# Query features of the late token blocks as four 32-row matmul groups in a decoder layer on Trainium2

## The chip, the cores and the metric

The kernel runs on one core of one Trainium2 chip, as one launch. The metric is the device time of that launch in microseconds (us), taken from timed runs. A separate profiled execution gives the traces that are read here. Engines are named as in the profile: PE is TensorE (PEld its weight loads), DVE VectorE, ACT ScalarE, POOL GpSimd, and SP the engine that issues most DMAs.

## What is computed

A decoder layer in float32 over `x` of 2 x 2048 tokens with 512 features: linear attention with a random feature map, then cross attention to a context of 154 keys, then a mixture of experts, each on a layer norm of its input and added to it. The part that matters is the first:

```python
def _elu1(x):
    return jnp.where(x > 0, x + 1.0, jnp.exp(x))
qkv = x @ w_qkv
q, k, v = jnp.split(qkv, 3, axis=-1)            # to 16 heads of 32
q_proj = _elu1(jnp.einsum('bhnd,hdf->bhnf', q, proj_matrix))   # 32 -> 128
k_proj = _elu1(jnp.einsum('bhnd,hdf->bhnf', k, proj_matrix))
kv = jnp.einsum('bhnf,bhnd->bhfd', k_proj, v)
attn = jnp.einsum('bhnf,bhfd->bhnd', q_proj, kv)
k_sum = k_proj.sum(axis=2)
z = 1.0 / (jnp.einsum('bhnf,bhf->bhn', q_proj, k_sum) + 1e-08)
out = (attn * z[..., None]).transpose(0, 2, 1, 3).reshape(b, n, d)
return out @ w_out + b_out
```

## The kernel before

The 4096 tokens are eight blocks `b` of 512 (`TB`); blocks 0 to 3 are the first batch and 4 to 7 the second, which are called the late blocks here. The 16 heads are four chunks `c` of four heads, so a chunk is 128 rows of features by 512 tokens.

Products are kept exact by splitting each operand into a high part in the type `float32r` and a low part, the remainder. `TERMS` names the three products that are summed: high by high, low by high, high by low. A full product over 128 rows thus is three matmuls (`product`, L148). For a head's features only 32 rows are contracted, so the three terms are stacked instead: `stack` (L292) loads a chunk's queries from DRAM (`qd`, which holds the high and the low part) three times, by three DMAs, into 96 partitions (high, low, high) of `qst`; `pst` holds `proj` in the order (high, high, low). One matmul of 96 rows then sums the three terms of one head (`query_features`, L479), into one bank `pqp` of the PSUM pool `sc`, which has four banks.

`features` turns a bank into `e_q`: two operations on ScalarE (L364, L365: relu and exp of the negated value), one on VectorE (L366), after which the bank is free. `numerators` and `denominators` multiply `e_q` with `kv` and with the key sums by plain float32 matmuls of 32 columns, the four heads each in its own quarter of the array's columns (`columns.matmul`, L230; `pn` and `pd`). `columns.matmul` also keeps the order of these among themselves as written.

Dense work (`Dense`) is a list of generators that give one matmul at a step; loops call `dense.fill(n)` to put n of them between the steps of the latency-bound work. Which instruction comes when on each engine is then settled by a scheduler when the program is built, engine by engine, from what is ready in its own estimate; each engine runs its list in order.

The first loop does the keys of all blocks and the queries of the early ones. The late blocks' queries run in a loop of 17 steps (L1346): per step one chunk's features, the chunk before it into `pn` and `pd`, a part of the attention output of earlier blocks (`attended`: POOL multiplies `num` by the reciprocals `zr` at L563, ScalarE casts the result to `at` at L564, VectorE takes the remainder at L118; `attention_out`: the matmuls `po_a`), and at the end the layer norm and the queries of the cross attention (`pt_x`, `xpq`). `xr_a` are tiles of `x` to which the output is added. Large tiles come from one pool of 17 buffers of 8 KB a partition (`eight`); a DMA into a tile waits for a free buffer. The DMAs of `qst`, `zr`, `xr_a` and the results all stand in SP's one queue.

Of the kernel before, what the change touches and what calls it, by code (L numbers as in the profile page):

```python
# [9 lines left out]
F32 = mybir.dt.float32  # L10
FR = mybir.dt.float32r
# [6 lines left out]
P = 128  # L18
D = 512
NC = D // P  # L20
H = 16
HD = 32
FEAT = 128
TB = 512
# [13 lines left out]
def decoder_layer(  # L38
# [26 lines left out]
    nc = tc.nc  # L65
    tokens = x.shape[0]
    nblk = tokens // TB
    bpb = nblk // batches
# [7 lines left out]
    sc = ctx.enter_context(tc.tile_pool(name="sc", bufs=SC, space=PSUM))  # L76
    dram = ctx.enter_context(tc.tile_pool(name="dram", bufs=1, space=DRAM))
    summed_up = ctx.enter_context(ExitStack())
    rows = ctx.enter_context(ExitStack())
# [18 lines left out]
    def eight(shape, dtype, name):  # L98
        return big.tile(shape, dtype, tag="b8", name=name)

    def half(name, dtype=F32):
        return work.tile([P, 512], dtype, tag="kp", name=name, bufs=9)
# [13 lines left out]
    def low(dst, src, hi, eng=None):  # L116

        (eng or nc.vector).tensor_tensor(dst, src, hi.bitcast(F32), ALU.subtract)  # L118

    def load_weight(w, name):  # L120
        raw = eight([P, NC, w.shape[1]], F32, f"raw_{name}")
        for k in range(NC):
            nc.sync.dma_start(out=raw[:, k], in_=w[k * P : (k + 1) * P, :])
        return [raw[:, k] for k in range(NC)]

    def split_weight(raw, name, busy=False):

        hi = eight([P, NC, D], FR, f"{name}_hi")
        lo = eight([P, NC, D], FR, f"{name}_lo")
        for k in range(NC):  # L130
            if isinstance(raw, list):
                part = raw[k]
            else:
                part = load_tile(raw, 0, k, name)
            if busy:
                nc.gpsimd.tensor_scalar(hi[:, k], part, 1.0, None, ALU.mult)
            else:
                nc.scalar.copy(hi[:, k], part)
            low(lo[:, k], part, hi[:, k], nc.gpsimd if busy or k % 2 else nc.vector)
        return hi, lo  # L140

    TERMS = ((0, 0), (1, 0), (0, 1))
# [90 lines left out]
    columns = Columns()  # L233

    def fl(k, f):
        return int((k + 1) * f + 1e-6) - int(k * f + 1e-6)
# [27 lines left out]
    def layernorm(d, b, at, xts, name):  # L264


        made = {}

        def values(t):
            if t == 0:  # L270
                xts[b] = new_xt(f"{name}{b}")
            made[t] = normalize(load_tile(d, at, t, f"{name}{b}_"), f"{name}{b}_{t}")
            yield from ()

        def turn(t):
            transposed(made.pop(t), xts[b], t, f"{name}{b}_{t}")
            yield
            yield

        return [values(t) for t in range(NT)], [turn(t) for t in range(NT)]  # L280
# [4 lines left out]
    def load_tile(d, b, t, name):  # L285
        xs = work.tile([P, D], F32, tag="xs", name=f"xs{name}{b}_{t}", bufs=5)
        nc.sync.dma_start(out=xs, in_=tile_of(d, b, t))
        return xs
# [3 lines left out]
    def stack(dst, d, parts=(0, 1, 0)):  # L292
        for r, part in enumerate(parts):
            nc.sync.dma_start(
                out=dst[r * HD : (r + 1) * HD].bitcast(F32),
                in_=d[part].rearrange("(h d) n -> d h n", d=HD),
            )
# [33 lines left out]
    raw = wk  # L331
    wk = [eight([P, NC, D], FR, f"wk_{i}") for i in ("hi", "lo")]
    for t in range(NT):
# [5 lines left out]
        b = nc.vector.tensor_tensor(lo, pt, hi.bitcast(F32), ALU.subtract)  # L339
        c = nc.scalar.copy(wk[0][:, t], raw[t])  # L340
        d = (nc.gpsimd if t % 2 else nc.vector).tensor_tensor(wk[1][:, t], raw[t], wk[0][:, t].bitcast(F32), ALU.subtract)
# [7 lines left out]
    low(pst[rest], praw[rest], pst[rest])  # L349
    wq = split_weight(load_weight(w_qkv[:, :D], "wq"), "wq")  # L350

    kvs, kszs, pkvs, kaccs, made_kv = [], [], [], [], []
    qd = [[dram.tile([2, P, TB], F32, name=f"qd{b}_{c}") for c in range(NC)] for b in range(nblk)]
    stks, vas, kps = {}, {}, {}
# [6 lines left out]
    def features(src, name, e=None):  # L361

        e = half(f"e_{name}") if e is None else e
        nc.scalar.activation(e, src, AF.Relu, scale=-1.0)  # L364
        nc.scalar.activation(e, e, AF.Exp, scale=-1.0)  # L365
        nc.vector.scalar_tensor_tensor(e, src, 0.0, e, ALU.max, ALU.add)  # L366
        return e
# [102 lines left out]
    qsts, qps, pds, nums, numd, zrs, zds, ats = {}, {}, {}, {}, {}, {}, {}, {}  # L470

    def load_queries(b, c):
        qsts[b, c] = eight([3 * HD, 4, TB], FR, f"qst{b}_{c}")
        stack(qsts[b, c], qd[b][c])

    def query_features(b, c, h):
        head = slice((4 * c + h) * FEAT, (4 * c + h + 1) * FEAT)
        pp = sc.tile([P, TB], F32, tag="sc", name=f"pqp{b}_{c}_{h}")
        nc.tensor.matmul(pp, lhsT=pst[:, head], rhs=qsts[b, c][:, h, :], start=True, stop=True)  # L479
        e = None  # L480
        if b < bpb and h:
            e = early.tile([P, TB], F32, tag="eq", name=f"eq{b}_{c}_{h}")
        qps[b, c, h] = features(pp, f"q{b}_{c}_{h}", e)

    def numerators(b, c):
        if c == 0:
            if b < bpb:
                numd[b] = dram.tile([P, NC, TB], F32, name=f"numd{b}")
            else:
                nums[b] = eight([P, NC, TB], F32, f"num{b}")  # L490
        pn = bank(f"pn{b}_{c}")
        for h in (3, 2, 1, 0):
            columns.matmul(
                pn[h * HD : (h + 1) * HD, :],
                lhsT=kvs[b // bpb][:, 4 * c + h, :],
                rhs=qps[b, c, h],
                start=True,
                stop=True,
            )
        if b < bpb:  # L500
            num = half(f"num{b}_{c}")
            nc.vector.tensor_copy(num, pn)
            dense.after(8, lambda: nc.sync.dma_start(out=numd[b][:, c], in_=num))
        else:
            nc.vector.tensor_copy(nums[b][:, c], pn)
# [42 lines left out]
    def load_reciprocals(b, c):  # L548
        two = pair_of(f"zr{b}_{c}").bitcast(F32)
        for h in range(4):  # L550
            nc.sync.dma_start(
                out=two[h * HD : (h + 1) * HD],
                in_=zds[b][h : h + 1, c : c + 2].to_broadcast([HD, 2, TB]),
            )
        for i in range(2):
            zrs[b, c + i] = two[:, i]
# [18 lines left out]
    def attention_outs(b):  # L575
        return [attention_out(b, t) for t in range(NT)]
# [190 lines left out]
    for s in range(ws_gate.shape[1] // F):  # L767
# [9 lines left out]
        out=before,  # L777
        in_=before,
# [527 lines left out]
    for n in range(nblk * per):  # L1306
        b, c, t = n // per, n // NT % NC, n % NT
# [32 lines left out]
            load_queries(*chunks[bpb * NC])  # L1340

    wout = split_weight(w_out, "wout")
    steps = chunks[bpb * NC :]

    ahead = {n if n < 13 else n + 2: ((n - 1) // 2, (n - 1) % 2 * 2) for n in range(1, 15)}
    for n in range(len(steps) + 1):  # L1346
        if n < len(steps):
            b, c = steps[n]
            if n + 1 < len(steps):
                load_queries(*steps[n + 1])  # L1350
        if n + 1 in ahead:
            load_reciprocals(*ahead[n + 1])
        if n == 7:
            ln, tr = layernorm(x1[0], 0, 0, qts, "x")
            dense.add(*ln[:3])
            ln = ln[3:]
        if n == 8:
            dense.add(*tr[:1], *ln, *tr[1:])
        if n == 11:
            dense.add(*(cross_query(0, i) for i in range(NC)))  # L1360
        for i in range(2):
            if n < len(steps):
                query_features(b, c, 2 * i)
                query_features(b, c, 2 * i + 1)
            dense.fill(fl(2 * n + i, 13 if n < 12 else 14))
            if n in ahead:
                attended(ahead[n][0], ahead[n][1] + i)
                if ahead[n][1] and i:
                    whole = ahead[n][0]
                    if whole < nblk - 2:  # L1370
                        dense.add(*attention_outs(whole))
                    if whole + 1 < bpb:
                        load_numerators(whole + 1)
            if n and i:
                columns.batch()
                numerators(*steps[n - 1])
                denominators(*steps[n - 1])
        if n == 10:
            xwq = split_weight(wq_t, "xwq")
        if n == 11:  # L1380
            open_early.clear()
            attending.close()
            res = attending.enter_context(tc.tile_pool(name="res", bufs=1))
            for i in range(NC):
                load_keys(0, i)
# [3 lines left out]
    steps = [(b, c, t) for b in range(nblk) for c in range(NC) for t in range(NT)]  # L1389
    for n in range(len(steps) + LAG + 1):  # L1390
        if n < len(steps):
            b, c, t = steps[n]
# [44 lines left out]
        if n > LAG:  # L1437
            b, c, t = steps[n - LAG - 1]
# [47 lines left out]
    for n, (group, u) in enumerate(todo3):  # L1486
# [14 lines left out]
        if n == LAST:  # L1501
            f0, f1 = finished(g, 0), finished(g, 1)
            d = downs
# [115 lines left out]
```

## Time and profile before

| | |
|---|---|
| timed runs, median of 3 | 2338.83 us (2337.85 to 2339.55) |
| profiled execution, its own time | 2335.7 us |
| span of its instructions | 2333.9 us |
| granted TensorE clock, mean | 0.986 |
| busy: PE, DVE, ACT, POOL | 96%, 72%, 47%, 53% |
| the 128 matmuls of L479, first and last start | 232.3 and 632.7 us |
| DMA, whole span | 498.23 MB |

A busy time is the sum of what an engine's instructions cover. Matmuls are pipelined: one starts before the one before it has ended, so a matmul's price in a stream is the distance between starts and not its length. Half of the matmuls of L479 are those of the late blocks; they lie from about 480 us on.

### The profile page before, as it was taken

To read this page: it belongs to the slowest core of one execution; us is meant where nothing else is said; L and a number is where in the kernel's file an instruction comes from. 1 tells how busy PE (TensorE), PEld (TensorE's weight loads), DVE (VectorE), ACT (ScalarE), POOL (GpSimd) and SP (SyncE) were. 2 spreads that over 40 slices of the span, in tenths; PEclk is the share of its full clock that TensorE was granted. 3 is DMA by queue.
4 is the path that set the end of the run, shared out by engine and by line. 5 is a ranking of instruction groups with operands and counts; after the bars stand their busy time and mean duration, and the time that the engine had idled before them with its cause. 6 is when DMAs were issued, how large, how long until landed. Compare 5 with 4: busy or idle time off the path is not lost.

```text
span 2333.9 us, 35151 instructions
## 1 busy us (share of the span) xinstructions
PE 2237.3 (96%) x11978; PEld 1733.5 (74%) x11978; DVE 1682.5 (72%) x2733; ACT 1104.6 (47%) x2598; POOL 1225.4 (53%) x1078
## 2 busy tenths in 40 slices
PE   7999999898899999999999999999999999999998
PEld 6888777655566776766787877888878888788887
DVE  6554555578577776778977777787797877877776
ACT  4555676756466766775343343222433223332221
POOL 5545433547475565553765554555484554755543
PEclk9999999999999999999999999999999999999999
DMA  6555778899974665566866657665557656575553
GB/s 212 181 171 173 208 210 228 241 260 263 255 211 141 172 179 159 166 197 218 293 235 229 241 184 299 225 225 221 176 193 294 242 211 233 180 280 207 203 191 129
DMA packets 201810, 498.23 MB, mean 213 GB/s; under 512 B 27739, under 2 KB 47579, under 8 KB 181695
## 3 DMA queue, kind: packets, MB, share of 16 engines
q1 hardware_dynamic: 199902, 489.89, 64.1%
q0 software_dynamic: 1728, 6.09, 0.9%
q8 instruction: 96, 1.57, 0.3%
q14 instruction: 84, 0.68, 0.1%
HBM read 351.30 MB, written 144.60 MB: 212 GB/s over the span
## 4 chain that ended last, share of the span: by engine, by line
PE 70%; DMA 13%; DVE 8%; POOL 3%; issue 3%; ACT 2%; SPq 1%; DVEq 0%; POOLq 0%; ACTq 0%
PE pg L1082 28%; PE pf L1195 11%; PE pk L148 3%; PE pq L148 3%; PE pv L148 3%; PE pf L148 3%; PE po_x L148 3%; PE xpq L148 3%; PE pp L402 2%; PE pc L745 2%; PE xpt L725 2%; PE pkv L230 1%; PE psc L693 1%; DMA zr<-zd 1%; DMA wds<-wdq 1%
## 5 line engine op out<-in xcount | busy, mean ns | idle before, releaser
L1082 PE MATMUL pg<-xo,wq 128*128 128x512 f32 x3360 | 826.0, 392 | 4.0 <-DMA wq<-wqs 1.1
L1082 PEld LDWEIGHTS pg<-xo,wq 128*128 128x128 f32 x3360 | 629.8, 188 | 145.6 <-ACT s L1093 3.4
L1216 DVE TENSOR_TENSOR sum<-sum,pf 128x512 f32<-128x512 f32 x376 | 250.7, 682 | 50.2 <-PE pf L1195 43.5
L407 POOL TENSOR_TENSOR kacc<-kacc,e_k 128x512 f32<-128x512 f32 x128 | 166.1, 1298 | 226.2 <-DVE e_k L366 204.5
L703 ACT ACTIVATE xe<-psc,nb 128x154 f32<-128x154 f32 x512 | 194.7, 404 | 64.9 <-DVE nb L700 49.3
L708 POOL TENSOR_TENSOR xe<-xe,sm 128x616 f32<-128x616 f32 x128 | 156.9, 1234 | 107.9 <-DVE sm L707 71.5
L1195 PE MATMUL pf<-ht,wdo 128*128 128x512 f32 x696 | 188.4, 395 | 10.8 <-DVE sum L1216 10.8
L1145 POOL TENSOR_TENSOR u<-u,gr 128x512 f32<-128x512 f32 x48 | 65.6, 1368 | 238.4 <-DVE u L1114 237.1
L366 DVE SCALAR_TENSOR_TENSOR e_k<-pp,e_k 128x512 f32<-128x512 f32 x128 | 87.3, 684 | 107.4 <-ACT e_k L365 101.5
L1195 PEld LDWEIGHTS pf<-ht,wdo 128*128 128x128 f32 x696 | 130.8, 189 | 41.4 <-DVE sum L1216 12.1
L1195 PE MATMUL pf<-hb,wdo 128*128 128x512 f32 x522 | 148.3, 399 | 0.0
L1113 ACT ACTIVATE u<-u 128x512 f32<-128x512 f32 x80 | 50.6, 633 | 201.7 <-DVE u L1102 201.4
L148 PE MATMUL pf<-wd,hp 128*128 128x512 f32 x528 | 133.6, 400 | 4.7 <-DVE mv_n L248 3.4
L700 DVE TENSOR_REDUCE nb<-psc 128x2 f32<-128x308 f32 x256 | 111.8, 467 | 32.5 <-PE psc L693 32.2
L148 PEld LDWEIGHTS pf<-wd,hp 128*128 128x128 f32 x528 | 99.4, 190 | 32.9 <-issue 6.3
L1102 DVE TENSOR_TENSOR u<-u,pg 128x512 f32<-128x512 f32 x160 | 108.3, 680 | 10.2 <-PE pg L1082 9.0
L1195 PEld LDWEIGHTS pf<-hb,wdo 128*128 128x128 f32 x522 | 98.2, 189 | 22.4 <-DVE sum L1216 0.8
L703 ACT ACTIVATION_READ_ACCUMULATOR xe<-psc,nb 128x1 f32 x512 | 111.5, 218 | 0.0
L364 ACT ACTIVATE e_k<-pp 128x512 f32<-128x512 f32 x128 | 76.8, 601 | 71.0 <-PE pp L402 62.8
L693 PEld LDWEIGHTS psc<-xkst,xst 96*128 96x128 f32 x512 | 76.5, 194 | 37.1 <-ACT xe L703 16.8
L693 PE MATMUL psc<-xkst,xst 96*128 96x154 f32 x512 | 90.4, 285 | 13.4 <-ACT xe L703 7.3
L402 PEld LDWEIGHTS pp<-pst,kst 96*128 96x128 f32 x512 | 75.7, 191 | 25.2 <-issue 8.6
(285 smaller groups left out, 5131.9 us busy)
## 6 DMA issues: line engine op xcount, KB each, us to landing
wq<-wqs SPq DMA_DIRECT2D x90, 1024.0 KB
wqs<-wq SPq DMA_DIRECT2D x30, 1024.0 KB
wdo<-wds SPq DMA_DIRECT2D x29, 1024.0 KB
kst<-kd SPq DMA_DIRECT2D x96, 256.0 KB
qst<-qd SPq DMA_DIRECT2D x96, 256.0 KB
xst<-xqd SPq DMA_DIRECT2D x96, 256.0 KB
wdo<-wds SPq DMA_DIRECT2D x29, 768.0 KB
kd<-khl SPq DMA_DIRECT2D x32, 512.0 KB
```

The lines of the kernel that those rows point to most:

```text
L148: nc.tensor.matmul(dst, lhsT=a, rhs=b, start=n == 0, stop=n == len(todo) - 1)
L366: nc.vector.scalar_tensor_tensor(e, src, 0.0, e, ALU.max, ALU.add)
L402: nc.tensor.matmul(pp[:, h], lhsT=stks[b, c][:, h, rows], rhs=pst[:, head], start=True, stop=True)
L407: nc.gpsimd.tensor_tensor(acc, acc, kp, ALU.add)
L693: nc.tensor.matmul(psc[:, i], lhsT=xsts[b, c][:, h, t * P : (t + 1) * P], rhs=ksts[bt, c][:, h, :], start=True, stop=True,)
L700: nc.vector.tensor_reduce(nb[:, two], psc, AX.X, ALU.max, negate=True)
L703: nc.scalar.activation(e[:, h, :], psc[:, i], AF.Exp, bias=nb[:, h : h + 1], accum_out=sm[:, h : h + 1],)
L708: nc.gpsimd.tensor_tensor(e, e, sm.unsqueeze(2).to_broadcast([P, 4, keys]), ALU.mult)
L1082: nc.tensor.matmul(pb, lhsT=w[:, p, i, k, :], rhs=xop[:, q, k, :], start=first and m == 0, stop=m == len(todo) - 1, skip_group_check=True,)
L1102: nc.vector.tensor_tensor(dst, dst, pb, ALU.add)
L1195: nc.tensor.matmul(banks[i], lhsT=w[:, p, i * P : (i + 1) * P], rhs=t[q], start=new and m == 0, stop=m == len(TERMS) - 1, skip_group_check ...
L1216: nc.vector.tensor_tensor(dst, dst, banks[i], ALU.add)
```

## The change

The late blocks' queries are no longer stacked. One DMA per chunk loads the pair (high, low) as it lies, 128 partitions by two parts by 512 tokens, and two chunks share one buffer (`qh`). Head `h` of a chunk then lies in partitions 32 h to 32 h + 31. `load_rows` makes a second copy of `proj` laid out in the same way, as high and low part (`prows`). `chunk_features` computes a chunk's four heads by twelve matmuls of 32 rows, three terms by four heads, each head in its own quarter of the array's rows and into its own bank, in the order term by term. All twelve are given at the first of a step's two halves; before, two heads were given in each half. The early blocks keep `query_features`.

```diff
+    def load_rows():
+
+        raw = eight([P, NC, FEAT], F32, "prow")
+        for h in range(4):
+            nc.sync.dma_start(
+                out=raw[h * HD : (h + 1) * HD],
+                in_=proj.rearrange("d (c h f) -> d h c f", c=NC, h=4)[:, h],
+            )
+        pair = eight([P, 2, NC, FEAT], FR, "prows")
+        nc.scalar.copy(pair[:, 0], raw)
+        low(pair[:, 1], raw, pair[:, 0], nc.gpsimd)
+        prows.append(pair)
...
     def load_queries(b, c):
+        if b >= bpb:
+            if c % 2 == 0:
+                two = eight([P, 2, 2, TB], FR, f"qh{b}_{c}")
+                for i in range(2):
+                    qsts[b, c + i] = two[:, i]
+                    nc.sync.dma_start(
+                        out=two[:, i].bitcast(F32), in_=qd[b][c + i].rearrange("r p n -> p r n")
+                    )
+            return
         qsts[b, c] = eight([3 * HD, 4, TB], FR, f"qst{b}_{c}")
         stack(qsts[b, c], qd[b][c])
...
+    def chunk_features(b, c):
+
+        pps = [sc.tile([P, TB], F32, tag="sc", name=f"pqp{b}_{c}_{h}") for h in range(4)]
+        for n, (i, j) in enumerate(TERMS):
+            for h in range(4):
+                rows = slice(h * HD, (h + 1) * HD)
+                columns.matmul(
+                    pps[h],
+                    lhsT=prows[0][rows, i, c, :],
+                    rhs=qsts[b, c][rows, j, :],
+                    start=n == 0,
+                    stop=n == 2,
+                    skip_group_check=True,
+                )
+        for h in range(4):
+            qps[b, c, h] = features(pps[h], f"q{b}_{c}_{h}")
...
     wout = split_weight(w_out, "wout")
+    load_rows()
     steps = chunks[bpb * NC :]
...
         for i in range(2):
-            if n < len(steps):
-                query_features(b, c, 2 * i)
-                query_features(b, c, 2 * i + 1)
+            if n < len(steps) and i == 0:
+                chunk_features(b, c)
             dense.fill(fl(2 * n + i, 13 if n < 12 else 14))
```

## The prediction

> **What bounds the kernel now.** I read the page's totals first, then the windows of the stage that is edited, then who waits there, then TensorE's timeline for the price of each kind of matmul.
>
> ```profile
> PE 2237.3 (96%) x11978; PEld 1733.5 (74%) x11978; DVE 1682.5 (72%) x2733; ACT 1104.6 (47%) x2598; POOL 1225.4 (53%) x1078
> ```
>
> TensorE is busy for 96% of the span, so time added to or taken from its stream anywhere reaches the end nearly one to one. The late blocks' query features run from about 490 to 640 us (windows view: stretch and its length, busy us of PE, PEld, DVE, ACT, POOL with counts, granted clock, DMA share, GB/s):
>
> ```profile
> 490.00:640.00 150.00, 136.13 (x687) 82.99 (x687) 104.50 (x159) 87.41 (x161) 82.85 (x75) 0.99 0.93 254
> ```
>
> Here TensorE stands still for 150.0 - 136.1 = 13.9 us, and the DMA engines are busy 0.93 of the time, against 0.65 over the span (the queues' shares on the page). The waits of this stretch (total us, times, longest):
>
> ```profile
> ACT at L564 <- POOL num L563: 30.5, 13, 6.6
> POOL num L563 <- DMA zr<-zd: 29.7, 4, 17.1
> ...
> PEld pqp L479 <- DVE e_q L366: 14.8, 14, 3.3
> ...
> PE pqp L479 <- DVE e_q L366: 8.1, 7, 2.5
> ```
>
> The reader sees a chain: late transfers (zr) hold POOL, POOL holds ScalarE's cast `at`, and the query features queued behind that cast free their banks late, so the next pqp matmul waits 8.1 us in all on TensorE. The prices come from TensorE's timeline (start, length, line, operation, count):
>
> ```profile
> 512.90 0.61 PE L148 MATMUL po_a<-wout_hi,at 128*128 128x512 f32 x2
> 513.36 0.39 PE L148 MATMUL po_a<-wout_lo,at 128*128 128x512 f32 x1
> 513.58 0.39 PE L148 MATMUL po_a<-wout_hi,at 128*128 128x512 f32 x1
> 513.90 1.06 PE L230 MATMUL pn<-e_q,kv 128*32 128x512 f32 x8
> 514.78 1.04 PE L230 MATMUL pd<-e_q,ksz 128*32 128x512 f32 x8
> 515.75 0.50 PE L148 MATMUL po_a<-wout_hi,at 128*128 128x512 f32 x1
> 516.09 0.40 PE L479 MATMUL pqp<-qst,pst 96*128 96x512 f32 x1
> 516.33 0.40 PE L148 MATMUL po_a<-wout_lo,at 128*128 128x512 f32 x1
> ```
>
> Starts count, not lengths. Full-array matmuls follow each other at 0.23 us, and the 96-row pqp is one of them (516.09 to 516.33 is 0.24). Going over to the column-tiled pn costs 513.90 - 513.58 = 0.32, that is 0.09 more. Eight of these (4 heads in 2 passes) take 0.88. Coming back costs 515.75 - 514.78 = 0.97, again 0.09 more, and the first matmul after it takes 0.34 to the next start, 0.11 more, since its weights were not loaded ahead. That tiles do run at once is seen in an earlier stretch of the same timeline:
>
> ```profile
> 481.56 0.63 PE L230 MATMUL pn<-eq,kv 128*32 128x512 f32 x3
> 481.58 0.62 PE L230 MATMUL pn<-e_q,kv 128*32 128x512 f32 x1
> 482.01 0.60 PE L230 MATMUL pn<-eq,kv 128*32 128x512 f32 x3
> ```
>
> Four start within 0.02 us, the next round 0.45 later.
>
> **Removed.** The 64 stacked pqp of the late blocks: 64 x 0.23 = 14.7 us of TensorE. Also 48 loads of 256 KB.
>
> **Added on TensorE.** 192 matmuls of 32 rows. No row of the trace shows a row-tiled one; bounds are four at once (0.23 a round, as the column tiles do) and one after another (0.23 each). I take the first, since the nearest row is the column-tiled one. In the order in which the built program issues them, the 192 do not stand in 16 blocks of twelve: they stand in 38 runs, 16 of nine to twelve, one of three and 21 single ones between po_a, pt_x or xpq matmuls, because each goes out when its bank is due. A long run still has three rounds: 16 x 3 x 0.23 = 11.0. The 22 short ones hide nothing: 22 x 0.23 = 5.1. The whole program's changes of tiling go from 288 to 341, 53 more. A change costs 0.09 of emptying and 0.11 of weights not loaded ahead, 0.20 together: 53 x 0.20 = 10.6. The bounds of this are 0 (rows of the array may need no emptying) and 0.20. Sum: 11.0 + 5.1 + 10.6 - 14.7 = +12.0 us.
>
> One rule would make it worse. The weight loads of pn stand together (start, length, count):
>
> ```profile
> 636.61 0.16 PEld L230 LDWEIGHTS pn<-e_q,kv 128*32 128x32 f32 x8 [0.35 <-issue]
> 637.07 0.13 PEld L230 LDWEIGHTS pd<-e_q,ksz 128*32 128x32 f32 x4 [0.30 <-issue]
> ```
>
> One lasts 0.11 (median 110 ns in the tile view of `ksz`), so four within 0.13 us are not one after another, and I let row tiles load at once too. The Trainium skill ("TensorE: Matmul & The Clock Gate", LDWEIGHTS) gives a load P / 1.2 ns with P its columns, 107 ns for 128 columns whatever the rows; twelve in series would be an estimated 1.28 us a chunk against the 0.92 removed. The same page (Measured speedup vs the span model) gives four row tiles of K=32, N=512 a speedup of 3.07 and not 4, an estimated 12 x 0.23 / 3.07 = 0.90 us a chunk in place of 0.69, which would add 3.4 us. No run here shows either.
>
> **Loads.** 16 of 512 KB and four of 64 KB for the rows of `proj` take the place of 48 of 256 KB: 12.6 to 8.7 MB, 3.9 of the stage's 38.14 MB:
>
> ```profile
> DMA packets 19844, 38.14 MB, mean 254 GB/s; under 512 B 3733, under 2 KB 3925, under 8 KB 19449
> ```
>
> At 0.93 x 150 = 139.5 us for 38.14 MB that is 14 us of DMA time, a share of 0.84. SP issues 28 loads fewer at 0.43 us each (median of qst in its line's view), and they stood ahead of zr and xr_a in its queue. What TensorE gets of it is bounded by 0 and its 13.9 us of standing; I take 4, half of the 8.1 that hang on late features, since the column of waits starts at zr but POOL's own 1.43 us per num remains.
>
> **Banks and features.** All four banks fill together, in the third round. ScalarE then has 8 operations at about 0.53 start to start (4.2 us), VectorE 0.68 after the last: 4.9 us until the fourth bank is free, 5.6 with the rounds. A chunk lasts 10.2 us now (pn at 503.79 and 13 chunks later at 636.61), so this is covered, except where the casts `at` come between: in the new order four stand in a row on ScalarE, paced by POOL (4 x 1.43 = 5.7), behind waits that now reach 6.6. What is queued behind the waiting cast is the next chunk's features, and behind those the pqp runs and all of TensorE. Two chunks need 2 x 5.6 + 5.7 - 1.2 = 15.7 of 20.4, which leaves 4.7; waits of 5 to 6.6 exceed it by 0.3 to 1.9. That is about what pqp waits today: I book 0 and keep 8 either way.
>
> **The first chunks.** Before, three matmuls of chunk (4,0) go out by 479.7. Now all twelve stand behind the second group of sums (491.9). Between them and (4,1) lie 12 xpv matmuls (2.8 us), then only 16 sums passes (1.8): with 4.9 needed each time TensorE waits 2.1 + 3.1 = 5.2, against 1.7 now (1.02 and 0.68 before the pqp at 496.3 and 497.5). +3 us. The copy and subtraction for `prows` (0.6 on ScalarE, 1.3 on POOL) lie before that beside other work; uncovered they cost 1.9. The bigger buffer costs nothing: two slots were cycling for qst, and prows takes the one that pst frees.
>
> **Sum.** +12.0 - 4 + 3 = +11 us on the profiled execution's 2335.7 us (span 2333.9): 2346.7. The three timed runs have their median 3.1 above that execution: about 2350; I write 2349.
>
> **Rivals.**
> 1. Faster: the changes of tiling are free for rows, and the lighter DMA queue decides. TensorE then pays 11.0 + 5.1 - 14.7 = +1.4, +3 at the start, and the waits give back up to 12: -8, 2331. For it: 0.93 DMA share and waits that begin at zr. Against it: the 0.09 at each change to columns. It decides from the point where a change costs below 0.05 us (53 x 0.05 = 2.7). 0.17.
> 2. No change: free or half-priced changes and 4 to 6 us back from the waits: 2336 to 2342. 0.17.
> 3. Rows in series (the change doesn't do what it says): 192 x 0.23 + 10.6 - 14.7 = +40, less 1 for the rest: 2378. Against it: the four starts within 0.02 us. 0.10.
> 4. My case, 2344 to 2366: 0.56.
>
> **The numbers.** About 0.2% (4.7 us) is what a measurement can tell from no change: faster is below 2334.2, slower above 2343.5. Slower is 0.56 + 0.10. The range runs from rival 1's 2331 to 2368, which is my case with the 3.4 and the 8 of late features added and part of the relief lost; left out are most of the serial case and a gain beyond 8.
>
> **What would show it.** Right: in the stretch that replaces 490 to 640, TensorE's timeline has pqp runs of twelve in about 0.7 us, single ones that cost 0.6 from the matmul before to the matmul after, DMA share near 0.84, and waits of pqp on e_q of 5 to 13 us. Wrong: starts 0.23 apart within one round (rival 3), single pqp with 0.23 on both sides (rival 1), or the waits on zr gone with the standing time under 5 us.

## The result

| | median | runs | TensorE busy | DMA moved |
|---|---|---|---|---|
| before | 2338.47 us | 2337.85 to 2339.55 | 2237.3 us | 498.23 MB |
| after | 2364.08 us | 2358.73 to 2369.06 | 2257.1 us | 494.30 MB |

The changed kernel takes 1.0113 of the time before, with a 95% interval of 1.0096 to 1.0129: 25.6 us more. The profiled execution of after took 2369.06 us (span 2367.3) and is the longest of its four; against the profiled one before (2335.7, span 2333.9) it is 33.4 us longer, so a difference between the two traces shows somewhat more than the medians do.

The page's totals after:

```profile
PE 2257.1 (95%) x12106; PEld 1737.2 (73%) x12106; DVE 1681.2 (71%) x2733; ACT 1101.7 (47%) x2599; POOL 1222.9 (52%) x1079
```

TensorE is busy 19.8 us longer and stands 13 us longer. The other engines do what they did. The windows view of the stage that was 490 to 640, now 497.5 to 677 (stretch and length, busy us of PE, PEld, DVE, ACT, POOL, granted clock, DMA share, GB/s):

```profile
497.50:677.00 179.50, 156.51 (x819) 87.80 (x818) 109.93 (x173) 86.81 (x167) 82.62 (x81) 0.92 0.65 203
```

The DMA share fell from 0.93 to 0.65, further than the 0.84 forecast, and yet TensorE stands for 23.0 us in place of 13.9. And the granted clock, 0.99 before, is 0.92. Two timeline excerpts of TensorE (start and length in us, line, operation, tiles, count) show the edit itself, a run of twelve and a single:

```profile
592.94 0.39 PE L148 MATMUL po_a<-wout_lo,at 128*128 128x512 f32 x1
593.26 0.97 PE L230 MATMUL pqp<-qh,prows 32*128 32x512 f32 x12
594.16 1.07 PE L230 MATMUL pn<-e_q,kv 128*32 128x512 f32 x8
...
529.99 0.61 PE L148 MATMUL po_a<-wout_hi,at 128*128 128x512 f32 x2
530.53 0.50 PE L230 MATMUL pqp<-qh,prows 32*128 32x512 f32 x1
530.96 0.50 PE L148 MATMUL po_a<-wout_lo,at 128*128 128x512 f32 x1
531.30 0.62 PE L148 MATMUL po_a<-wout_hi,at 128*128 128x512 f32 x2
```

Twelve take 0.90 from their start to the start of what follows: the four of a round start within 0.01 us, the second round 0.34 after the first, the third 0.23 after that, and `pn` 0.33 after the third. The single stands where two po_a would have gone on at 0.23: the second po_a of the first pair started at 530.22 (0.23 after the first), and the next but one after it starts at 531.30, which is 1.08 for what would take 0.46 without the pqp. It costs 0.62, and the prediction's 0.23 + 2 x 0.20 is 0.63.

### The profile page after: what moved, and what is told of

The parts are those of the page before. It is cut to its first block, busy times and chain, and to the rows that moved or that the text cites. A ratio compares the mean times of both kernels' runs of the same rounds, so it can differ in the third digit from the quotient of the medians.

```text
span 2367.3 us, 35401 instructions
## 1 busy us (share of the span) xinstructions
PE 2257.1 (95%) x12106; PEld 1737.2 (73%) x12106; DVE 1681.2 (71%) x2733; ACT 1101.7 (47%) x2599; POOL 1222.9 (52%) x1079
## 2 busy tenths in 40 slices
DMA packets 199825, 494.30 MB, mean 209 GB/s; under 512 B 27290, under 2 KB 47642, under 8 KB 179710
## 4 chain that ended last, share of the span: by engine, by line
PE 57%; DVE 5%; DMA 4%; POOL 2%; issue 2%; ACT 1%; SPq 1%; DVEq 0%; POOLq 0%; ACTq 0%
PE pg L1123 29%; PE pf L1236 11%; PE pf L148 4%; PE po_x L148 3%; PE xpq L148 3%; PE pc L786 2%; PE psc L734 2%; PE xpt L766 2%; DMA wds<-wdq 1%; DMA xr_x<-x 1%; DMA xst<-xqd 1%; PE tail L767 0%; PE ptf L846 0%; DVE nb L741 0%; DVE u L1143 0%
## 5 line engine op out<-in xcount | busy, mean ns | idle before, releaser
L1236 PE MATMUL pf<-ht,wdo 128*128 128x512 f32 x696 | 188.9, 397 | 10.9 <-DVE sum L1257 10.9
L734 PEld LDWEIGHTS psc<-xkst,xst 96*128 96x128 f32 x512 | 75.9, 192 | 34.9 <-ACT xe L744 15.4
L148 PE MATMUL po_x<-xwo_hi,cx 128*128 128x512 f32 x256 | 87.0, 413 | 9.1 <-DVE cx L118 3.8
```

The lines of the kernel that those rows point to most:

```text
L148: nc.tensor.matmul(dst, lhsT=a, rhs=b, start=n == 0, stop=n == len(todo) - 1)
L734: nc.tensor.matmul(psc[:, i], lhsT=xsts[b, c][:, h, t * P : (t + 1) * P], rhs=ksts[bt, c][:, h, :], start=True, stop=True,)
L1236: nc.tensor.matmul(banks[i], lhsT=w[:, p, i * P : (i + 1) * P], rhs=t[q], start=new and m == 0, stop=m == len(TERMS) - 1, skip_group_check ...
```

## Where the 25 us went

TensorE's waits from 470 to 700 us show what is new (waiting line, releaser: us in total, times, longest):

```profile
PE pqp L230 <- DVE e_q L381: 7.6, 6, 3.8
PE pn L230 <- DVE xr_a L315: 6.7, 1, 6.7
PE ptks L474 <- DVE ks L470: 5.7, 1, 5.7
PE psc L734 <- DVE e_q L381: 4.4, 2, 2.5
PE po_a L148 <- DVE xr_a L315: 4.3, 3, 3.0
```

The first line is the wait that the prediction watched, and it is no longer than before (8.1). The wait on `ks` is new, and it is the easiest to follow back. VectorE's timeline, before and then after (the bracket is the idle time ahead of the group and what ended it):

```profile
479.83 0.69 DVE L455 COPY ks<-pks 128x512 f32<-128x512 f32 x1 [1.15 <-PE pks L447]
481.27 2.80 DVE L118 TENSOR_TENSOR at<-num,at 128x512 fp32r<-128x512 f32 x2 [0.74 <-ACT at L564]
```

```profile
483.24 2.77 DVE L118 TENSOR_TENSOR at<-num,at 128x512 fp32r<-128x512 f32 x2 [2.53 <-ACT at L605]
485.93 0.68 DVE L470 COPY ks<-pks 128x512 f32<-128x512 f32 x1
```

Before, the copy of `ks` stands ahead of the remainders of `at`; after, behind two of them. Nothing in the diff touches either: the scheduler, planning the whole program again, put them the other way round. `at` waits for ScalarE's cast, that for POOL's `num`, and that for a transfer:

```profile
481.29 2.48 POOL L604 TENSOR_TENSOR num<-num,zr 128x512 f32<-128x512 f32 x2 [2.06 <-DMA zr<-zd]
...
482.59 0.62 ACT L605 CAST at<-num 128x512 fp32r<-128x512 f32 x1 [3.83 <-POOL num L604]
```

So `ks`, whose bank was filled at 481.0, is copied at 485.9, and TensorE, in its own timeline, stands and then runs slowly:

```profile
486.66 1.12 PE L474 MATMUL ptks<-ident,ks 128*128 128x128 f32 x4 [5.69 <-DVE ks L470]
487.71 1.07 PE L230 MATMUL pn<-eq,kv 128*32 128x512 f32 x3
...
488.56 1.07 PE L230 MATMUL pn<-eq,kv 128*32 128x512 f32 x3
```

The same rounds of pn started 0.45 apart before (481.56, 482.01); here it is 0.85. The 6.7 us wait of pn (565.4 to 572.1) has the same shape: the addition to `xr_a`, which frees the bank of po_a that pn waits for, stands on VectorE behind two remainders of `at`, and these behind a cast that waited 9.77 us for POOL's `num`.

```profile
568.71 2.75 DVE L118 TENSOR_TENSOR at<-num,at 128x512 fp32r<-128x512 f32 x2 [9.46 <-ACT at L605]
571.38 0.68 DVE L315 TENSOR_TENSOR xr_a<-xr_a,po_a 128x512 f32<-128x512 f32 x1
```

POOL in its turn waited 6.79 us for a load (`num` from `numd`). The DMA engines were busy 0.91 of the time from that load's issue (556.4) to the end of POOL's wait (566.8), and 0.99 of the time from 475.0 to 481.3, where POOL's wait for the `zr` of the first case ended. The stage's mean of 0.65 hides that these late transfers moved while the engines were nearly full. The windows view of the stretch of `ks`, and of the one around the end of the wait of pn, gives the granted clock, third column from the end:

```profile
485.70:492.50 6.80, 5.84 (x23) 1.80 (x24) 4.24 (x10) 2.09 (x4) 1.44 (x1) 0.50 0.81 190
567.60:577.80 10.20, 5.69 (x21) 2.33 (x22) 8.82 (x11) 6.50 (x12) 10.20 (x8) 0.50 0.37 120
```

The trace lists the granted clock in stretches of some 3.4 us or multiples, each at 1.00 or 0.50. That allows one account for every kernel. **Standing** is the time from the start of the span to the end of TensorE's last matmul in which it is not busy. **Half clock** is half of its busy time inside stretches at 0.50. **Work** is busy time less half clock. The profiled executions give:

| | work | standing | half clock |
|---|---|---|---|
| before | 2209.3 | 92.9 | 28.0 |
| after | 2218.6 | 105.9 | 38.5 |
| difference | +9.3 | +13.0 | +10.5 |

Only the first difference was in the prediction's sum with about its right size (+12.0). By the same account nearly all of this lies between 440 us and the first matmul of the experts (`pg`, at 1046.2 before and 1079.8 after): standing there is 48.7 before and 61.5 after, half clock 13.8 and 23.4, work 543.6 and 554.9. From there to the end the two kernels agree to within 0.5 us in each. The half clock of a single execution is uncertain by several us: the granted clock of the kernel before lies between 0.979 and 0.987 in 17 executions on one chip. As an estimate from the means of all executions (0.9808 for after, 0.9838 to 0.9846 for the kernel before on four chips), one minus the clock times the span, the missing clock is 8 to 10 us more after.

## Experiments

Theory A: the stream of TensorE costs what the prediction said, and the rest is standing behind reordered queues plus half clock after it. Theory B, later D: four banks filled at once hold the features up. Theory C: the row-tiled matmuls cost more than 0.23 a round. All ratios are to the kernel before on the same chip, five rounds each; where an expectation is in us, it is compared by its ratio to 2338.5. The scheduler plans every version anew, so each pair compares two whole plans.

### One suspect at a time

**Four heads at once, without row tiles.**

```diff
-            if n < len(steps):
-                query_features(b, c, 2 * i)
-                query_features(b, c, 2 * i + 1)
+            if n < len(steps) and i == 0:
+                for h in range(4):
+                    query_features(b, c, h)
```

> The kernel before (2338.5 us) with one edit: the four stacked query features of a late chunk are issued together at the start of its step, instead of two and two. No row tiles, loads as before. Theory A (TensorE's stream pays about 12 us for row runs and changes of tiling, and the rest of the loss is standing time behind reordered queues): VectorE's copy of ks stays ahead of the at remainders here, and there are as many changes of tiling as before (288), so 2338 to 2344. Theory B (filling four banks together is what holds the features up): most of the 25.6 us are here already, 2350 to 2364. Theory C (the row-tiled matmuls themselves cost more than the 0.23 a round that I took): like A, 2338 to 2344.

Measured: 2345.21 us, ratio 1.0013 (1.0000 to 1.0026). The batch alone, in the order that this version got, costs some 3 us. That is the size of the prediction's start-up term, and B's 12 us or more are not there.

**`ks` ahead of `at`.** `issue_after` puts instructions behind a named one in its engine's queue, without a wait.

```diff
-        nc.vector.tensor_copy(ks, pks)
+        ks_done.append(nc.vector.tensor_copy(ks, pks).ins)
...
-        low(ats[b][1][:, c], at, ats[b][0][:, c])
+        with tc.issue_after(ks_done[-1]):
+            low(ats[b][1][:, c], at, ats[b][0][:, c])
```

> The changed kernel (2364 us) with the at remainders on VectorE held behind the copy of ks, as they stood in the kernel before; nothing else. Theory A: the 5.7 us for which ptks waited on ks at 481 to 487 us go, and with them the slow matmuls after it (six rounds at 0.85 in place of 0.43, 2.5 us): 2364 - 6 to 8 = 2356 to 2358. Theory B and C: that standing only moves to the next wait, since the features or the row runs set the pace: 2361 to 2365.

Measured: 2361.66 us, ratio 1.0087 (1.0070 to 1.0104). ptks waits 0.87 in place of 5.69, and standing falls from 105.9 to 92.8, but half clock is 44.3. The ratio is 0.0026 (6 us) below after's, though the two intervals overlap. It lies between A's range (1.0075 to 1.0083) and that of B and C (1.0096 to 1.0113), and its interval touches both, so the time decides nothing here.

**Whole runs.** The first of the twelve also waits for the last features before it:

```diff
+        last = freed[-1].name          # VectorE's last operation of the features traced before
         pps = [sc.tile([P, TB], F32, tag="sc", name=f"pqp{b}_{c}_{h}") for h in range(4)]
...
+                if n == h == 0:
+                    tc.add_manual_dep(m.ins, last, WHOLE, reason="whole run")
```

> The changed kernel with one wait more: the first of a chunk's twelve row-tiled matmuls also waits until the last of the previous features is done, so that all four banks are free and the twelve go out in one run. In the order as built that makes 16 runs of twelve in place of 38, and 296 changes of tiling in place of 341. Theory A by the prediction's prices: 45 changes x 0.20 + 22 short runs x 0.23 = 14.1 us less on TensorE (busy time 2257 to about 2243), so 2350, and up to 2356 if the run now waits for its banks. Theory B: the later start of a run costs what the shorter stream saves: 2360 to 2370, with more waits of pqp on e_q. Theory C: only some 5 us go (the short runs), since the price sits in the twelve themselves: 2359.

Measured: 2356.23 us, ratio 1.0067 (1.0047 to 1.0087), 11 us less than after. TensorE's totals:

```profile
PE 2241.5 (95%) x12106; PEld 1733.7 (74%) x12106; DVE 1679.2 (71%) x2733; ACT 1102.0 (47%) x2599; POOL 1222.9 (52%) x1079
```

Busy time fell by 15.6 us, work by 13.5, where the prices of the prediction give 14.1: C, which gave 5, falls. Standing is 107.0. One wait makes up 9 us of it; the timelines of POOL, ScalarE, VectorE and TensorE in turn:

```profile
645.67 2.48 POOL L610 TENSOR_TENSOR num<-num,zr 128x512 f32<-128x512 f32 x2 [9.61 <-DMA x<-xr_a]
...
646.96 0.62 ACT L611 CAST at<-num 128x512 fp32r<-128x512 f32 x1 [7.25 <-POOL num L610]
647.49 1.14 ACT L383 ACTIVATE e_q<-e_q 128x512 f32<-128x512 f32 x2
...
647.61 1.08 DVE L119 TENSOR_TENSOR at<-num,at 128x512 fp32r<-128x512 f32 x1 [6.50 <-ACT at L611]
...
652.16 1.65 PE L231 MATMUL pqp<-qh,prows 32*128 32x512 f32 x12 [9.07 <-DVE e_q L384]
```

Two of the four exp of the chunk (L383) are queued behind one cast of `at`, which POOL delivers 7 us later.

**Both.**

> Both edits on the changed kernel: whole runs of twelve, and ks ahead of the at remainders. Theory A: the sums add, 2364 - 14 - 7 = 2343, to 2350 where runs wait for banks; then the row tiles are worth 0 to +10 us against the kernel before. Theory B: 2356 to 2364. Theory C: 2352, the sum of 5 and 7.

Measured: 2363.45 us, ratio 1.0082 (1.0064 to 1.0100). This is a miss of A (2343 to 2350) and lies in B's range. The sums do not add: work is 2205.3 as in whole, ptks waits 0.87, and pqp waits 21.8 us on e_q in place of 17.8. In the new plan other waits took the place of the one that went.

### A rule for the order of the queues

If what stands at the head of ScalarE's and VectorE's queues is the cause, a rule should help that no single wait explains: cast and remainder of `at` go behind the features of the chunk traced before them.

```diff
-        nc.scalar.copy(ats[b][0][:, c], at)
-        low(ats[b][1][:, c], at, ats[b][0][:, c])
+        with tc.issue_after(behind[0]), tc.issue_after(behind[1]):   # last exp, last addition
+            nc.scalar.copy(ats[b][0][:, c], at)
+            low(ats[b][1][:, c], at, ats[b][0][:, c])
```

On after, on whole, and on the kernel before:

> The changed kernel with one rule on the order of two queues: the cast of at on ScalarE and its remainder on VectorE are issued behind the features of the chunk traced before them, not ahead of them. Theory A (the loss that TensorE's stream does not explain, some 13 us of standing and 10 of half clock after it, comes from at waiting at the head of these queues for POOL's num): the waits on ks at 481 (5.7 us) and of pqp on e_q (7.6 us) shrink to 3 or less in sum, half of the half clock goes, 2364 to 2346 to 2352. Rival D (four banks that fill in the last round make the next run wait, whatever stands in the queues): pqp on e_q keeps its 7 us, only the wait on ks goes, 2356 to 2360. Rival E (the wait is moved, not taken): the standing turns up at po_a on at, 2360 or more.

> The same rule on the version with whole runs of twelve (ratio 1.0067 to the kernel before, where pqp waits 17.8 us on e_q, 9.1 of them at 643 behind at, and ptks 6.8 on ks). Theory A: 15 to 20 us go, so 0.998 to 1.001 of the kernel before. Rival D: only the 6.8 of ks and the slow clock after it, 1.003 to 1.005. Rival E: 1.006 or more, with po_a waiting on at.

> The same rule on the kernel before. It has 8.1 us of pqp waiting on e_q and no wait on ks. Theory A: 4 to 8 us less, 0.9965 to 0.9985 of the kernel before; then row tiles with whole runs are at par with stacked features or 2 to 4 us behind them once both have this order. Rival D: two banks a half step give the queues room enough, no change, 0.999 to 1.001. Rival E: slower, 1.002 or more, by waits at po_a.

Measured: 2357.73, 2347.36 and 2339.21 us; ratios 1.0075 (1.0057 to 1.0093), 1.0038 (1.0025 to 1.0051) and 1.0001 (0.9989 to 1.0014). On after, the waits that A named shrink (from 13.3 to 5.1 us in sum: ptks 0.87, pqp on e_q 4.2; A had said 3 or less), the standing by 10.8 us, half clock not at all, and the ratio by 9 us: D's number, not A's, since psc now waits 9.4 us. The kernel before gains nothing, though pqp waits 2.8 us in place of 8.1: another miss of A. On whole the ratio is D's as well (1.003 to 1.005), and one wait is left that is as long as the one before it. VectorE's and TensorE's timelines:

```profile
642.89 0.69 DVE L246 BATCH_NORM_STATS2 st_x<-xsx 128x6 f32<-128x512 f32 x1 [10.91 <-DMA xsx<-x]
...
648.32 0.68 PE L744 MATMUL psc<-xkst,xst 96*128 96x154 f32 x2 [11.38 <-POOL sd_x L251]
```

The releaser named for psc, POOL's sd_x, came last by the profile, but psc writes a bank that e_q has to free, and four e_q additions stand on VectorE behind st_x, a reading of the next stage's first tile, whose load is still under way.

**The twelve done twice** (on whole), the second pass writing the same sums again:

```diff
-        for n, (i, j) in enumerate(TERMS):
+        for n, (i, j) in enumerate(TERMS + TERMS):
...
-                    start=n == 0,
-                    stop=n == 2,
+                    start=n % 3 == 0,
+                    stop=n % 3 == 2,
```

> The version with whole runs (ratio 1.0067), where the twelve matmuls of each run are done twice, the second pass writing the same sums again: 192 row-tiled matmuls more and no more changes of tiling. Four at once (my price): 16 x 0.69 = 11.0 us more busy time on TensorE, up to 16 x 0.90 = 14.4 by the rows of the changed kernel's trace, in which twelve take 0.90 from start to next start; ratio 1.011 to 1.013. One after another (rival 3 of the prediction): 16 x 12 x 0.23 = 44 us, ratio 1.025.

Measured: 2399.76 us, ratio 1.0259 (1.0244 to 1.0273), 45 us above whole, which is rival 3's number. But the timeline refutes rival 3:

```profile
526.52 1.66 PE L231 MATMUL pqp<-qh,prows 32*128 32x512 f32 x24
528.11 0.49 PE L149 MATMUL po_a<-wout_hi,at 128*128 128x512 f32 x1
```

Twenty-four take 1.59 to the next start, 0.69 more than twelve, three rounds of 0.23. Work rose by 8.9 us, standing by 33.6 and half clock by 7.4; the longest waits are two of pqp on e_q (8.4 and 15.7) and one of po_a (12.6).

### Holding the second queue too

st_x (in `normalize`) is put behind the last features traced:

```diff
+        elif behind[1] is not None and in_late[0]:
+            tc.add_manual_dep(stats.ins, behind[1].name, ORDER_ONLY, reason="behind the features")
```

and in one version the first late chunk's run is issued ahead of the last group of sums (`load_rows` moves ahead with it, and step 0 of the late loop then has no run):

```diff
+        if m == (nblk - bpb) * per + NT - 1:
+            chunk_features(*chunks[bpb * NC])
```

> The version with whole runs and at behind the features (ratio 1.0038), and now also the first reading of the later stage's layer norm (st_x on VectorE, which waits for a load from DRAM) behind the features traced before it. In that version st_x waited 10.9 us at 632 to 643 for its load, four feature additions stood behind it, and TensorE waited 11.4 us for their banks, then ran at half clock for 17 us. Theory A: that wait and its half clock go, 2347 - 11 - 6 = 2330, ratio 0.996 to 0.999; TensorE's own work (busy less half-clock loss) stays at 2202 to 2205 us against 2209 of the kernel before. Rival D (four banks at once cost what they cost, wherever it shows): 1.002 to 1.004, with the wait under another name.

> The kernel before with both rules of order (at and st_x behind the features). With the first alone it stood at 1.0001. Theory A: it has no wait of 10 us of this kind to lose, so 0.998 to 1.000. Rival D: the same. If it gains as much as the row-tiled version, the order is worth that much to any version and the row tiles nothing.

> Both rules on the version with the twelve matmuls done twice. Without the rules the second pass cost 45 us (1.0067 to 1.0259) though its matmuls took only 16 x 0.70 = 11.2: the rest was 8.4 and 15.7 us of pqp on e_q and 12.6 of po_a on at, and half clock. Theory A: with the order held the second pass costs its matmuls alone, all_whole + 11 to 15 us, ratio 1.001 to 1.005. Rival D or a rival F (the row-tiled matmuls hold up something else, by their banks or their reads): still 30 us or more above all_whole.

> all_whole, and the first late chunk's run is issued ahead of the last group of sums instead of behind it, so that its four banks come free about 2 us earlier. In the version with at behind the features the second and third runs waited 5.6 and 1.5 us for their banks (494 to 507), against 1.7 in the kernel before; the prediction gave the start-up 3 us in all. Theory A: 2 to 4 us less than all_whole. Rival: the sums behind it and the run of the second chunk trade places only, the same as all_whole within 2 us.

Measured: 2350.90, 2352.17, 2369.73 and 2345.50 us; ratios 1.0038 (1.0023 to 1.0053), 1.0049 (1.0032 to 1.0065), 1.0128 (1.0105 to 1.0151) and 1.0025 (1.0010 to 1.0040). The ratio of all_whole is D's (1.002 to 1.004) and not A's, and all_before misses the range that both gave it (0.998 to 1.000). In all_whole the 11.4 us of psc are gone (0.45 and 0.74 are left), and 10.9 stand elsewhere:

```profile
572.38 1.97 PE L266 MATMUL pt_x<-ident,xsx 128*128 128x128 f32 x8 [10.88 <-DVE xsx L259]
```

This one was made by the edit. The rule also held back the first block's layer norm, whose transposes pt_x stand in the middle of TensorE's stream; the kernel before got the same wait from it (11.2 us) and 0.0048 of time. The earlier first run is worth 3 us by the ratios, whose intervals overlap. The second pass now costs 21 us in place of 45, still more than A's 15 and less than F's 30.

So the rule is kept from the second block on (`in_late` is set at step 11 of the loop):

> Whole runs, at behind the features, and st_x behind the features from the second block of the later stage on; the first block's st_x stays where it stood (held back as well, it made pt_x wait 10.9 us on TensorE at 561 to 572, as long as the wait it had removed at 637). Theory A: both waits are gone, 11 us of standing and some 8 of half clock less than the versions at 1.0038: ratio 0.996 to 0.999. Rival D: a third wait of the same size turns up, 1.002 to 1.005.

> fin_whole with the first late chunk's run ahead of the last group of sums. The second and third run waited 4.3 us so, against 7.7 behind it. Theory A: 2 to 4 us less than fin_whole, 0.995 to 0.998, and the fastest of all. Rival D: 1.001 to 1.004.

> The kernel before with the same two rules of order. With at behind the features alone it stood at 1.0001; with the first block's st_x held back too at 1.0049, with pt_x waiting 11.2 us at 570. Theory A: 0.998 to 1.001, 2 to 6 us behind the row-tiled fin_whole, since TensorE's own work is 4 to 7 us more. Rival: the order alone is worth as much here, 0.996 to 0.998, and the row tiles nothing.

> fin_whole with the twelve matmuls done twice. Theory A: the second pass costs its 16 x 0.70 = 11.2 us, up to 15 with half clock: 1.001 to 1.005, that is 0.005 to 0.006 above fin_whole. Rival F (they hold up something else): 0.010 or more above fin_whole.

> The changed kernel with the two rules of order only, without the wait that makes whole runs. As built its row matmuls stand in 40 runs, 24 of them of one to three, with 346 changes of tiling against 303 of fin_whole (0.9988). Theory A, by the prediction's prices: 43 x 0.20 + 24 x 0.23 = 14.1 us more than fin_whole, 1.0048, the standing time as in fin_whole. If the whole runs only helped by another order of waits: 1.000 to 1.002.

> The changed kernel with two heads to a half step, as before the change, and the two rules of order: six row-tiled matmuls a run in two quarters of the rows, so half the array idles and two banks fill at a time. TensorE's sum against fin_whole: 32 x 3 x 0.23 = 22.1 in place of 11.0, six split runs 1.4, 37 changes x 0.20 = 7.4, in all 20 us more. Theory A (the stream and the order are all there is): 0.9988 + 0.0085 = 1.007. Rival D (four banks at once make the features late): it gets back 7 us or more by shorter waits of pqp, 1.004 or less.

The last of these, two heads to a half step:

```diff
-    def chunk_features(b, c):
+    def chunk_features(b, c, hs):
...
-            if n < len(steps) and i == 0:
-                chunk_features(b, c)
+            if n < len(steps):
+                chunk_features(b, c, (2 * i, 2 * i + 1))
```

| | median | ratio | 95% | work | standing | half clock |
|---|---|---|---|---|---|---|
| fin_whole | 2336.92 | 0.9988 | 0.9977 to 0.9998 | 2204.3 | 92.7 | 42.4 |
| fin_early | 2336.69 | 0.9987 | 0.9976 to 0.9999 | 2204.6 | 86.9 | 35.9 |
| fin_before | 2343.55 | 1.0021 | 1.0007 to 1.0035 | 2207.9 | 95.2 | 33.2 |
| fin_doubled | 2368.61 | 1.0122 | 1.0102 to 1.0142 | 2215.0 | 104.1 | 38.2 |
| fin_after | 2344.95 | 1.0018 | 1.0007 to 1.0030 | 2220.5 | 83.4 | 36.6 |
| fin_two | 2363.51 | 1.0097 | 1.0075 to 1.0120 | 2223.4 | 109.4 | 34.9 |

(The profiled execution of fin_whole took 2345.5 us, the longest of its twelve, so its three columns add up to more than its median.)

fin_after is the change as it was drawn, with nothing but the order of two queues held: it is 4 us slower than before in place of 26. That is less than A's 1.0048, and in the range (1.000 to 1.002) that was given for the case that whole runs only help by another order of waits. Yet its work is 16.2 us above fin_whole's (14.1 expected), as A had it; what A had wrong is that the standing would stay, for it is 9.3 us less. That whole runs wait for the last of their banks, and so lose half of what they save, fits these columns but is not shown by a run of its own. With whole runs the version is 3 us below the kernel before, with an interval that just excludes zero; as the lowest but one of eighteen versions that is weak evidence of a gain. fin_early adds nothing that can be told from that, though the expectation had 2 to 4 us. These are the two fastest versions. The same order does not help the kernel before (1.0001, and 1.0021 where A had 0.998 to 1.001). fin_two's work is 19 us more than fin_whole's (20 expected). With two banks at a time pqp waits 3.3 us on e_q, against 6.2 in fin_whole and 4.4 in fin_after, whose edit differs from fin_two's only in giving four heads at once; so four banks at once cost 1 to 3 us here, about as much as in the first experiment, and the 7 us or more that D gave them are not there. The two longest waits of fin_two are po_a and pt_x behind the layer norm on VectorE (8.3 and 8.2 us), so its ratio, above both forecasts, says less than its work.

fin_doubled contradicts A in part. Its work is 10.7 us above fin_whole's (11.2 expected), its time 31 us by the ratios, which is rival F's condition (0.010 or more). Its two longest waits of TensorE are of the old kind with another tile, the addition that frees po_a's bank:

```profile
579.48 1.93 PE L232 MATMUL pn<-e_q,kv 128*32 128x512 f32 x8 [4.73 <-DVE xr_a L322]
663.39 1.93 PE L232 MATMUL pn<-e_q,kv 128*32 128x512 f32 x8 [7.04 <-DVE xr_a L322]
```

Whether that is again an order that no rule holds, or the later end of each run, stays open: no version was built in which the second pass left every queue as it was.

Over all versions, then, A's prices gave the changes of work to within 3 us, and its times came true in four of the eighteen (batch_only, whole, early_whole, fin_whole). The standing moved from plan to plan by more than A allowed.

## Why the prediction was right or wrong

The sum was +11 us, and 25.6 were measured. Its term for TensorE's stream holds; what failed is the standing, booked at -1, and the half clock, not booked.

**TensorE's stream: right.** Its term was +12.0 us. The work column holds it apart from all waits, and it repeats over versions whose matmuls differ little but in order:

| versions | work, mean | difference | from the prediction's prices |
|---|---|---|---|
| stacked features (before, batch_only, pin_before, all_before, fin_before) | 2209.5 | | |
| row tiles in 38 or 40 runs (after, ks_first, pin_after, fin_after) | 2220.6 | +11.1 to stacked | +12.0 |
| row tiles in 16 whole runs (seven versions) | 2205.0 | -15.5 to 38 or 40 runs | -14.1 |
| twelve done twice (three versions) | 2215.4 | +10.4 to whole runs | +11.2 |

The members of a row lie within 7 us. So the sums made of 0.23 a round of four, 0.20 a change of tiling, and 0.23 for a single that hides nothing come out, and the rows above show the first (0.69 for a second pass of three rounds) and the single with its two changes (0.62) by themselves.

**The page's lower speedup: not found in these rows.** The Trainium skill ("TensorE: Matmul & The Clock Gate", Measured speedup vs the span model) gives 3.07 for four row tiles. Twelve more in a run took 0.69 here, which is a speedup of 4. Twelve alone take 0.90 to the next start, the same as the estimate from the page, but 0.20 of that is the change of tiling, already in the sum. The estimated 1.28 us for twelve weight loads in series is refuted by the same rows.

**Relief by fewer transfers: not isolated.** I gave it -4 us, and no run has the lighter loads alone. With the order held, fin_after stands 9.5 us less than the kernel before, at a DMA share of 0.74:

```profile
491.90:655.00 163.10, 154.19 (x823) 86.28 (x826) 105.30 (x162) 86.72 (x168) 78.86 (x74) 0.94 0.74 228
```

One wait does bear on the loads: with the order held, pqp of the stacked kernel waits for its own transfers (qst, 4.2 us in pin_before and 5.9 in fin_before), and in fin_after TensorE has no such wait. In after itself the share fell further and the standing grew. The mean says little about single transfers: the two loads behind the waits of ks and pn moved while the DMA engines were busy 0.99 and 0.91.

**First chunks: +3, near.** In after the second run waits 0.45 + 0.68 + 1.97 = 3.1 us for its banks, against 1.02 + 0.68 = 1.7 before, and pn of the third late chunk is 4.1 us further behind than pn of the first (515.28 - 503.79 = 11.5 against 497.52 - 490.16 = 7.4); 0.9 of these 4.1 are half clock.

**Banks and features: this step failed.** I wrote "I book 0 and keep 8 either way". I saw four casts of `at` in a row on ScalarE, saw that features queue behind them, and then weighed the lengths of the work (15.7 of 20.4 us) as if the order were the one before with four banks in place of two. That the late features alone cost nothing is even right: pqp waits 7.6 us on e_q against 8.1. What costs is what else the new plan put behind instructions with a late input: ks, pn and po_a behind `at` (5.7 + 6.7 + 4.3 us), and psc behind the readings `st_x` of the next stage's tiles (4.4), none of them named in the prediction. In the kernel before the largest sum beside the 8.1 of pqp is 4.2 us (psc on ScalarE's `xe`). Standing was booked at -4 + 3 + 0 = -1 and measured at +13.0.

**Half clock: not in the sum at all.** It is 10.5 us of the profiled difference. The column was in the windows line that I quoted (0.99), and I priced waits at their length. What sets its size stays open. It does not follow the standing: fin_whole stands as long as the kernel before (92.7 and 92.9) with 42.4 us of half clock against 28.0, and ks_first stands 13.1 less than after with 5.8 more of it. Nor does any run tell whether the row-tiled matmuls themselves have a part in it: the profiled versions with row tiles have 30 to 45 us, those with stacked features 28 to 38.

**My rivals.** Rival 3 (rows in series) is refuted by the starts within 0.01 us and by 0.69 for a second pass. Rival 1's condition (a change of tiling below 0.05 us) is refuted by the single that costs 0.62, that is 0.20 a change; its relief is not isolated. The total, 2364, came out inside the range I gave, near its upper end, which "late features" had been given 8 us for; the mechanism behind those 8 was not the one that took the time, so that the total lies there is luck.

## What to carry to other kernels

When a scheduler plans each engine's queue, an edit's price has two parts: its instructions, which could be priced from rows to within a few us here, and the new plan, which moved more here and is read by comparing the order of the queues before and after, for every instruction that lands behind one with a late input. Look there for work on the critical path (a copy out of a bank, an exp) that now stands behind work that waits for a transfer, and hold the order by hand before judging the edit: here that turned 26 us of loss into 4. A stop of TensorE can cost more than its length (the 5.69 us for `ks` were followed by work at half clock), but no fixed factor came out of these runs.

## What the runs showed of the hardware

- The granted clock went to 0.50 after or during stops and back after 3.4 us or a multiple (3.4, 6.8, 10.2, 13.7, 17.1, 20.5 us). It did not need one long stop: in after, with stops of 0.45, 0.68 and 1.97 us between 503.3 and 508.0, it was 0.50 from 506.2 to 513.0, and in the kernel before 1.02 and 0.68 us (495.3 to 497.5) were followed by 3.4 us of it, while a single stop of 2.4 us there (531) was followed by none. The Trainium skill ("TensorE: Matmul & The Clock Gate", What's actually happening) says that a free-running window of about 3.4 us is judged; the lengths agree. Its abstract rule of no idle gap above about 3.4 us (HAM oscillation — how this bites in real kernels) is too mild for these rows.
- Four row tiles of 32 rows run at once with `float32r` operands: starts within 0.01 us, rounds 0.23 apart at full clock and 0.43 at half.
- Going from row tiles over to column tiles costs what other changes cost: twelve pqp followed by pn take 0.90 for three rounds, 0.21 above 3 x 0.23, of which 0.11 come in the first round and 0.10 ahead of pn.
